# A graph network kernel: slot rows and block places fetched twice a group, and two product buffers in layer 0

## The chip, the cores and the metric

The kernel runs on 1 core of one Trainium2 chip. The metric is the device time of one execution in microseconds (us). The kernel before took 6175.32 us, the median of 6 runs (6166.19 to 6210.36).

A core has five engines that run their own instruction streams in order: PE (matrix products into PSUM; its weight loads are listed as PEld), DVE (vector work), ACT (scalar activations, copies, and here also the register work), POOL (here mainly indirect DMAs) and SP (here only DMA issues). PEq, ACTq and SPq are the sequencers of PE, ACT and SP: ACTq L1318 is a register load, SPq L1312 a DMA issue.

## The reference

Two message passing layers over the same 400,000 edges between 12,500 nodes of 32 features. The edges arrive sorted by destination. Each layer is followed by a residual sum and a layer norm.

```python
# layer 0: nine spline weights per edge, from edge_attr (two numbers per edge)
messages = jnp.einsum('ek,ei,kio->eo', basis, x[row], weight)      # 9 x 32 x 32
out = jnp.zeros(...).at[col].add(messages) / jnp.maximum(degree, 1.0)[:, None]
out = out + x @ root_w.T + root_b
x = _layernorm(x + out)
# layer 1: four weights per edge, from a table indexed by edge_type
for b in range(4):
    m = (x[src] @ W[b]) * edge_type_weight[b][edge_type][:, None]
    out = out + segment_sum(m, dst)
x = _layernorm(x + out)
```

## The kernel before

**Two ways to fetch x[src].** The edges are cut into 125 groups of 2304 (18 chunks of 128). Before the layers, the edges of each group are sorted by source on the chip. Layer 0 takes groups 33 to 124 (92 groups), layer 1 all 125: 217 in all. The rest of the edges is gathered row by row with indirect DMAs on POOL (tile `n_xg`, helper line L124): 28 gathers to a batch, one batch after the other, in both layers. This part is called "near" in the code (class `Near`).

**A group is fetched by products with one-hot matrices.** The 12,500 nodes form 98 windows of 128 nodes; 7 windows form a block, and a group has `NBL` = 14 blocks. For each block of each group there is a slot row of `WS` = 608 int16 numbers in DRAM (`slots`), which say which node of its window stands at each place. In `take(g)` the 14 blocks are cut into four `PIECES` of 3, 4, 3 and 4 blocks. For each piece, `block(k)`

- loads the slot rows into the tile `sl`, the same bytes to all 128 partitions (L1312, issued by SP);
- loads the block places, 3 or 4 int32 numbers, into `hd` on one partition (L1316, SP);
- reads these numbers into ACT's registers with one register load (L1318, ACTq TENSOR_LOAD), which is held behind the copy before last (`issue_after(moves[-2])`);
- compares the slots with the partition's own number on DVE, which gives the one-hot tile `s` (L1324).

Then for each block PE makes 7 products of node windows with the one-hot columns into one of three PSUM banks (`bank`, L1334), and ACT copies the bank into the group's row buffer `yt` at a place held in registers (L1341).

**A group is used in three steps of 6 chunks.** `use(g)` turns the rows to edges on PE (`y`, L1354) and, in `product(s)`, makes the outer products with the edge weights (tile `t`, one of `NOUT` tiles named `outer_i`; L1373 on ACT in layer 0, L584 on DVE) and the spread one-hot of the destinations (tile `hot`, a pool of `NOUT` buffers; L1374 on ACT and L1376 on DVE in layer 0, L1366 on DVE in layer 1). `add(s)` sums them on PE into `agg` (L1389); it is emitted `LAG` steps after its product. L603 copies `agg` out, L609 multiplies with the weights, L591 to L594 split the result into three bf16 parts, L746 adds them to the nodes. In layer 0 the first spline factor (`b0_ps`, L1240) lies in the same PSUM bank as `agg`.

**Buffers.** `NSRC` counts the `sl` tiles: 2 in layer 0 and 4 in layer 1, of up to 4 blocks each. `NONE` counts the `s` tiles: 3 and 5. `hd` has 2 buffers in both. Blocks of group g+1 are interleaved with the steps of group g, so fetching runs ahead of use by a group; an order within each engine is chosen by the framework's scheduler when the program is built, and each engine then runs it in order.

**Before the layers**, `counted()` works out the block places and writes them to `begin_d` in DRAM: 14 rows of 4 numbers a group, row k0 holding the places of the piece that begins at block k0 (one POOL memset, four DVE copies, one DMA).

Of the kernel before, what the change touches and what calls it, by code (L numbers as in the profile page):

```python
# [11 lines left out]
I16 = mybir.dt.int16  # L12
I32 = mybir.dt.int32
# [4 lines left out]
P = 128  # L18
# [4 lines left out]
def kernel(  # L23
# [38 lines left out]
    nc = tc.nc  # L62
# [3 lines left out]
    CH, NG, G0 = 18, 125, 33  # L66
# [29 lines left out]
    NBL = NW // B  # L96
# [13 lines left out]
    dram = ctx.enter_context(tc.tile_pool(name="dram", bufs=1, space=bass.MemoryType.DRAM))  # L110
# [21 lines left out]
    sort = phase0.enter_context(tc.tile_pool(name="sort", bufs=1))  # L132
# [45 lines left out]
    row = const.tile([P, 1], F32)  # L178
# [47 lines left out]
    def wide(name="wg"):  # L226
        return node_ps.tile([P, 4 * P], F32, name=name)
# [216 lines left out]
    WS = off_[B]  # L444
# [11 lines left out]
        signs(src_16, thr[:NG, w:w + 1], -1.0, counts[:NG, w:w + 1])  # L456

    PIECES = [(k * NBL // 4, (k + 1) * NBL // 4) for k in range(4)]
    PB = max(k1 - k0 for k0, k1 in PIECES)
    PW = PB * WS  # L460
    assert PB <= 4
    PAD = 512
    begin_d = dram.tile([NG, NBL, 4], I32, name="begin_d")
    seg = dram.tile([NG * NBL, 2], F32, name="seg")
    ROWS = TG * NBL
    NT = (NG + TG - 1) // TG
# [11 lines left out]
    def counted():  # L478
        nc.vector.tensor_scalar(counts[:NG, 1:NW], counts[:NG, 1:NW], 0.5, GE / 2, op0=ALU.mult,
                                op1=ALU.add)  # L480
        nc.vector.memset(counts[:, :1], 0.0)
        nc.vector.memset(counts[:, NW:], float(GE))
        out_, t = [sort.tile([P, NBL, B], F32, name=n) for n in ("outside", "rel_to")]
        far = sort.tile([P, 2], F32, name="far")
        firsts, ends = [counts[:NG, i:i + NW].rearrange("g (b j) -> g b j", j=B) for i in (0, 1)]
        anchors = firsts[:, :, BL:BL + 1].to_broadcast([NG, NBL, B])

        for c, to, f, op in ((firsts, out_, lo, ALU.is_lt), (ends, t, hi, ALU.is_gt)):
            nc.vector.tensor_tensor(to[:NG], c, anchors, op=ALU.subtract)
            nc.vector.tensor_tensor(to[:NG], to[:NG],  # L490
                                    f[:NG, None, :].to_broadcast([NG, NBL, B]), op=op)
        nc.vector.tensor_tensor(out_[:NG], out_[:NG], t[:NG], op=ALU.add)
        nc.vector.tensor_reduce(far[:NG, :1], out_[:NG].rearrange("g b j -> g (b j)"), axis=AX.X, op=ALU.add)
        far_ps = wide()
        nc.tensor.matmul(far_ps[:1, :1], far[:NG, :1], ones[:NG, :1], start=True, stop=True)
        nc.vector.tensor_tensor(unfit, unfit, far_ps[:1, :1], op=ALU.add)
        place = sort.tile([P, NBL], F32, name="place")
        nc.vector.tensor_tensor(place[:NG], firsts[:, :, 0], firsts[:, :, BL], op=ALU.subtract)
        nc.vector.tensor_scalar(place[:NG], place[:NG], float(AHEAD), 0.0, op0=ALU.add, op1=ALU.max)
        nc.vector.tensor_scalar(place[:NG], place[:NG], float(AHEAD), None, op0=ALU.min)  # L500

        nc.vector.scalar_tensor_tensor(place[:NG], firsts[:, :, 0], float(BANK), place[:NG],
                                       op0=ALU.mult, op1=ALU.add)
        p_i = sort.tile([P, NBL, 4], I32, name="p_i")
        nc.gpsimd.memset(p_i, 0)
        for k0, k1 in PIECES:
            n = k1 - k0
            nc.vector.tensor_copy(p_i[:NG, k0:k1, :n],
                                  place[:NG, None, k0:k1].to_broadcast([NG, n, n]))
        nc.sync.dma_start(begin_d.rearrange("g b i -> g (b i)"),  # L510
                          p_i[:NG].rearrange("g b i -> g (b i)"))
        sg = sort.tile([P, NBL, 2], F32, name="sg")
        nc.vector.tensor_scalar(sg[:NG, :, 0], firsts[:, :, BL], edges[:NG], None, op0=ALU.add)
        nc.vector.tensor_copy(sg[:NG, :, 1], node[:NG, :NW:B])
        nc.vector.tensor_scalar(sg[:NG, :, 1], sg[:NG, :, 1], row[:NG], None, op0=ALU.subtract)
        nc.sync.dma_start(seg.rearrange("(g b) i -> g (b i)", b=NBL),
                          sg[:NG].rearrange("g b i -> g (b i)"))
        nc.vector.memset(begin, 0.0)
        for t in range(NT):
            n = min(ROWS, NG * NBL - t * ROWS)  # L520
            nc.sync.dma_start(begin[:n, t, :], seg[t * ROWS:t * ROWS + n, :])
# [652 lines left out]

    def layer(which):

        NSRC, NONE, NOUT, LAG, NSUM = ((2, 3, 3, 1, 14), (4, 5, 4, 2, 18))[which]
        KK = K if which == 0 else NB
        GF = G0 if which == 0 else 0
        parts = x3[which][0]  # L1180
        with ExitStack() as stack:
            srcs = stack.enter_context(tc.tile_pool(name="srcs", bufs=NSRC))
# [3 lines left out]
            heads = stack.enter_context(tc.tile_pool(name="heads", bufs=2))  # L1186
# [112 lines left out]
            def take(g):  # L1299

                yt = yts[g % NYT]
                begins = {}
                ones_of = {}

                def block(k):
                    for k0, k1 in PIECES:
                        if k == k0:
                            n = (k1 - k0) * WS
                            sl = srcs.tile([P, PW], I16, name="sl")
                            r0 = g % TG * NBL  # L1310
                            a = slots[g // TG][r0 + k0:r0 + k1, :]
                            nc.sync.dma_start(sl[:, :n], bass.AP(tensor=a.tensor, offset=a.offset,  # L1312
                                                                 ap=[[0, P], [1, n]]))

                            hd = heads.tile([1, 4], I32, name="hd")
                            nc.sync.dma_start(hd, begin_d[g:g + 1, k0, :])  # L1316
                            with tc.issue_after(moves[-2].ins) if len(moves) > 1 else ExitStack():
                                _, v = nc.values_load_multi_w_load_instructions(  # L1318
                                    hd[:, :k1 - k0], engines=[mybir.EngineType.Activation],
                                    min_val=0, max_val=GE * BANK + AHEAD,  # L1320
                                    skip_runtime_bounds_check_because="counted, and bounded")
                            begins.update(zip(range(k0, k1), v))
                            s = ones_.tile([P, PW], BF16, name="s")
                            nc.vector.tensor_scalar(s[:, :n], sl[:, :n], row, None,  # L1324
                                                    op0=ALU.is_equal)
                            for i in range(k0, k1):
                                ones_of[i] = s[:, (i - k0) * WS:]
                    s = ones_of.pop(k)
                    bank = banks[(g * NBL + k) % len(banks)]
                    for j in range(B):  # L1330
                        a, b = at_[j]
                        w = k * B + j

                        nc.tensor.matmul(bank[:, AHEAD + a:AHEAD + b], parts[:, w * M3:w * M3 + P],  # L1334
                                         s[:, off_[j]:off_[j + 1]], start=(j == 0),
                                         stop=(j == B - 1), skip_group_check=True)
                    v = begins.pop(k)
                    to, place = [nc.s_assert_within(
                        e, 0, top, skip_runtime_bounds_check_because="counted, and bounded")
                        for e, top in ((v >> 9, GE), (v & (BANK - 1), AHEAD))]  # L1340
                    moves.append(nc.scalar.activation(  # L1341
                        yt[:M3, ds(to, LONG)], bank[:M3, ds(place, LONG)], AF.Copy))
                return [lambda k=k: block(k) for k in range(NBL)], yt

            def use(g, yt):
# [77 lines left out]
            for g in range(GF, NG + 1):  # L1423
# [6 lines left out]
                n, m = len(new), len(left)  # L1430
# [68 lines left out]
    for c in range(0, CH, 4):  # L1499
        n = min(4, CH - c)  # L1500
# [11 lines left out]
    ends[0][2].append(fallen)  # L1512
    phase0.close()
    layer(0)
    phase1.close()
    ends[1][2].append(near_fits)
    layer(1)
    again = const.tile([1, 1], I32)
    nc.vector.tensor_scalar(again, unfit, 0.5, None, op0=ALU.is_gt)
# [157 lines left out]
```

## Time and profile before

| what | value |
|---|---|
| median of 6 runs | 6175.32 us (6166.19 to 6210.36) |
| the profiled execution's own time | 6153.92 us |
| its span, first to last instruction | 6151.9 us |
| before layer 0 / layer 0 / change of layers / layer 1 | 0 to 880 / 880 to 3590 / 3590 to 3770 / 3770 to 6152 us |
| busy share of PE, PEld, DVE, ACT, POOL | 52, 44, 49, 35, 38% |
| mean granted PE clock | 0.739 of full speed |
| bytes moved by DMA | 565.07 MB, of which 511.82 MB on SP's queue |
| slot row loads | 868: 434 of 608 KB and 434 of 456 KB |
| gathers in batches | 1469 from x, 875 from `z_dram` |

A line of the groups gives the engine's busy time, the mean duration of one instruction in ns, and the idle time just before them with what ended most of it. In lines of waits the columns are: who waited at which line, for whom, us in total, times, longest. A line of a window gives its bounds, its length, the busy time and count of PE, PEld, DVE, ACT and POOL, the granted PE clock, the busy share of the 16 DMA engines and GB/s. A line of the timeline gives start, duration, engine, line, operation, tiles, count, and in brackets the idle time before it with the releaser.

### The profile page before, as it was taken

The numbers are of one execution on the slowest core, as the hardware profiler recorded it, in microseconds if no ns is written. First come the engines' busy times: TensorE is split into PE (matmuls) and PEld (weight loads), VectorE is DVE, ScalarE is ACT, GpSimd is POOL, SyncE is SP. The second block draws the span as 40 slices with busy tenths as digits, with TensorE's granted clock in tenths as the row PEclk, the third lists the DMA queues.
The fourth block names the chain that finished last, engine by engine and source line by source line (L and its number), as shares of the span: only waits on it lengthen the run. The fifth ranks groups of instructions, "written<-read, shape, count | busy, mean of one in ns | idle before, by whom it ended". The sixth has DMA issues, their size and how long they took to land.

```text
span 6151.9 us, 112981 instructions
## 1 busy us (share of the span) xinstructions
PE 3221.9 (52%) x40674; PEld 2690.5 (44%) x40674; DVE 3000.5 (49%) x5850; ACT 2154.1 (35%) x5610; POOL 2351.0 (38%) x2395
## 2 busy tenths in 40 slices
PE   1121135665556565556665664555555555555558
PEld 0111024444444444444444554555455555455547
DVE  3699685554445544334433443443443434444447
ACT  2577543333333333333333332322222223222324
POOL 5257743344433334433334213333333333333330
PEclk9955557777777777777777877777777777777779
DMA  3000023332223332222322333433333334333334
GB/s 61 6 11 15 13 86 95 94 90 86 83 84 94 91 95 82 85 81 88 89 88 78 102 112 106 126 116 114 108 117 112 110 114 121 114 114 115 118 115 144
DMA packets 266157, 565.07 MB, mean 92 GB/s; under 512 B 83608, under 2 KB 149756, under 8 KB 265086
## 3 DMA queue, kind: packets, MB, share of 16 engines
q1 hardware_dynamic: 187288, 511.82, 25.9%
q0 software_dynamic: 75888, 40.38, 4.8%
q8 instruction: 319, 5.23, 0.4%
q10 hardware_dynamic: 2410, 5.59, 0.3%
q14 instruction: 252, 2.06, 0.1%
HBM read 531.77 MB, written 25.78 MB: 91 GB/s over the span
## 4 chain that ended last, share of the span: by engine, by line
PE 37%; another core or an unknown queue 29%; issue 9%; ACT 4%; DVE 4%; DMA 1%; ACTq 1%; SPq 0%; POOL 0%; DVEq 0%
PE agg L1389 19%; PE bank L1334 12%; ACT yt L1341 2%; PE y L1354 2%; DVE outer L584 1%; PE n_bank L1083 1%; PE wg L880 1%; PE wg L609 1%; PE wg L1109 1%; DVE s L1324 1%; PE n_sum L746 1%; ACTq L1341 1%; DVE hot L1366 0%; ACT agg_sb L603 0%
## 5 line engine op out<-in xcount | busy, mean ns | idle before, releaser
L124 POOL DMA_INDIRECT n_xg<-in_x_dram,n_idx x1469 | 1479.8, 1007 | 1752.7 <-PE y L1354 453.0
L1334 PE MATMUL bank<-s,x 128*128 128x108 bf16 (+3 forms) x21266 | 1325.6, 210 | 1515.2 <-issue 903.1
L1334 PEld LDWEIGHTS <-x 128*128 128x128 bf16 x21266 | 1095.7, 103 | 1724.2 <-issue 1643.2
L1341 ACT ACTIVATE yt<-bank x3038 | 1165.9, 384 | 1667.9 <-remote 893.0
L1389 PE MATMUL agg<-hot,outer 128*128 128x82 f32 (+1 forms) x7812 | 1585.4, 347 | 238.7 <-issue 217.1
L124 POOL DMA_INDIRECT n_xg<-z_dram,near_i x875 | 842.5, 963 | 1658.1 <-PE n_bank L1083 830.3
L1389 PEld LDWEIGHTS agg<-hot,outer 128*128 128x128 f32 (+1 forms) x7812 | 1186.4, 198 | 426.6 <-issue 270.2
L1324 DVE TENSOR_SCALAR s<-sl,row 128x1824 bf16<-128x1824 int16 x868 | 669.8, 772 | 816.6 <-remote 521.3
L1366 DVE TENSOR_TENSOR hot<-in_order,y 128x492 f32<-128x492 bf16 x375 | 249.2, 665 | 691.4 <-remote 448.6
L1376 DVE TENSOR_TENSOR hot<-agg,hot_b 128x984 f32<-128x984 f32 x276 | 325.4, 1179 | 406.1 <-ACT agg_sb L603 150.4
L584 DVE TENSOR_TENSOR outer<-co,y 128x768 f32<-128x768 f32 x375 | 354.8, 946 | 0.0
L1354 PE MATMUL y<-add,yt 96*128 96x32 bf16 x3906 | 258.6, 180 | 173.6 <-DVE outer L584 115.5
L584 DVE TENSOR_TENSOR outer<-co_b,y 128x384 f32<-128x384 f32 x276 | 151.2, 548 | 311.4 <-ACT outer L1373 185.9
L1354 PEld LDWEIGHTS <-yt 96*128 96x128 bf16 x3906 | 207.9, 101 | 193.9 <-issue 187.7
L1374 ACT ACTIVATE hot<-hot_b 128x492 f32<-128x492 bf16 x276 | 167.5, 607 | 201.8 <-PE agg L1389 96.4
L1373 ACT ACTIVATE outer<-y 128x192 f32<-128x192 f32 x276 | 91.0, 330 | 405.8 <-remote 379.5
L1083 PE MATMUL n_bank<-n_w,n_xg 128*32 128x72 f32 x3024 | 112.7, 255 | 204.9 <-DVE n_w L1066 70.0
L245 ACT ACTIVATE in_order<-src,thr 125x2304 bf16<-125x2304 int16 x97 | 214.1, 2207 | 0.7
L603 ACT ACTIVATE agg_sb<-agg 128x82 f32<-128x82 f32 (+1 forms) x217 | 64.6, 298 | 416.3 <-remote 204.8
L743 DVE TENSOR_SCALAR n_hit<-cols,place_of 82x128 bf16<-82x128 f32 (+2 forms) x301 | 96.0, 331 | 198.7 <-remote 151.6
L591 ACT ACTIVATE rows<-wg 82x32 bf16<-82x32 f32 (+1 forms) x217 | 42.2, 194 | 384.6 <-remote 259.5
L609 PE MATMUL wg<-w_sb,agg_sb 97*82 97x33 f32 (+1 forms) x802 | 100.2, 245 | 139.7 <-ACT agg_sb L603 102.4
(267 smaller groups left out, 2991.6 us busy)
## 6 DMA issues: line engine op xcount, KB each, us to landing
sl<-slots SPq DMA_DIRECT2D x434, 608.0 KB
sl<-slots SPq DMA_DIRECT2D x434, 456.0 KB
n_xg<-in_x_dram,n_idx POOLq DMA_INDIRECT x1469
n_xg<-z_dram,near_i POOLq DMA_INDIRECT x875
hd<-begin_d SPq DMA_DIRECT2D x868, 0.0 KB
z_dram<-n_z SPq DMA_DIRECT2D x49, 256.0 KB
co_d<-co SPq DMA_DIRECT2D x13, 360.0 KB
co<-co_d SPq DMA_DIRECT2D x13, 360.0 KB
```

The lines of the kernel that those rows point to most:

```text
L124: return nc.gpsimd.indirect_dma_start(out=xg, out_offset=None, in_=table, in_offset=bass.IndirectOffsetOnAxis(ap=idx, axis=0))
L245: nc.scalar.activation(t, of[:NG], AF.Sign, bias=bias, scale=scale, accum_out=total)
L584: return nc.vector.tensor_tensor(t[:, :c, at:at + k * D].rearrange("p c (k d) -> p c k d", k=k), co[:, :, :, None].to_broadcast([P, c, k, D]),
L1083: nc.tensor.matmul(o, self.xg[i][:, at[0], at[1], :], v, start=True, stop=True, tile_position=(0, j * D))
L1324: nc.vector.tensor_scalar(s[:, :n], sl[:, :n], row, None, op0=ALU.is_equal)
L1334: nc.tensor.matmul(bank[:, AHEAD + a:AHEAD + b], parts[:, w * M3:w * M3 + P], s[:, off_[j]:off_[j + 1]], start=(j == 0), stop=(j == B - 1) ...
L1341: moves.append(nc.scalar.activation(yt[:M3, ds(to, LONG)], bank[:M3, ds(place, LONG)], AF.Copy))
L1354: nc.tensor.matmul(y[:, c, :], yt[:M3, k * P:(k + 1) * P], add3[:M3, :], start=True, stop=True)
L1366: nc.vector.tensor_tensor(hot.rearrange("p c (m i) -> p c m i", i=2), rel.to_broadcast([P, SUB, MAXR // 2, 2]), (col_ps if which else col_ ...
L1374: nc.scalar.activation(spread[:, :, 0, :], hot, AF.Copy)
L1376: nc.vector.tensor_tensor(spread[:, :, 1:, :], b0[:, :, :, None].to_broadcast([P, SUB, 2, MAXR]), hot[:, :, None, :].to_broadcast([P, SUB, ...
L1389: near.behind = nc.tensor.matmul(agg[0], t[:, c, :], v, start=(k == 0), stop=(k == CH - 1)).ins
```

## The change

Three things are changed.

1. Slot rows and block places are loaded in two halves of 7 blocks a group (`LOADS`), in both layers, instead of four pieces. A slot load is then 7 x 608 x 2 bytes x 128 partitions = 1,089,536 bytes, and a register load reads 7 numbers. `NSRC` is 2 in both layers, `hd` keeps 2 buffers. The one-hot compares still go by the four pieces; each reads its part of the half's tile.
2. `begin_d` becomes one row of 14 numbers a group, so the memset is dropped and one copy takes the place of four.
3. In layer 0 `NOUT` is 2 instead of 3: two tiles `outer_i` and two buffers of `hot` (the spread).

```diff
+    LOADS = [[(0, NBL // 2), (NBL // 2, NBL)]] * 2
-    begin_d = dram.tile([NG, NBL, 4], I32, name="begin_d")
+    begin_d = dram.tile([NG, NBL], I32, name="begin_d")
...
-        p_i = sort.tile([P, NBL, 4], I32, name="p_i")
-        nc.gpsimd.memset(p_i, 0)
-        for k0, k1 in PIECES:
-            n = k1 - k0
-            nc.vector.tensor_copy(p_i[:NG, k0:k1, :n],
-                                  place[:NG, None, k0:k1].to_broadcast([NG, n, n]))
-        nc.sync.dma_start(begin_d.rearrange("g b i -> g (b i)"),
-                          p_i[:NG].rearrange("g b i -> g (b i)"))
+        p_i = sort.tile([P, NBL], I32, name="p_i")
+        nc.vector.tensor_copy(p_i[:NG], place[:NG])
+        nc.sync.dma_start(begin_d[:, :], p_i[:NG])
...
-        NSRC, NONE, NOUT, LAG, NSUM = ((2, 3, 3, 1, 14), (4, 5, 4, 2, 18))[which]
+        NSRC, NONE, NOUT, LAG, NSUM = ((2, 3, 2, 1, 14), (2, 5, 4, 2, 18))[which]
...
-                ones_of = {}
+                ones_of, slots_of = {}, {}
 
                 def block(k):
-                    for k0, k1 in PIECES:
+                    for k0, k1 in LOADS[which]:
                         if k == k0:
                             n = (k1 - k0) * WS
-                            sl = srcs.tile([P, PW], I16, name="sl")
+                            sl = srcs.tile([P, max(b - a for a, b in LOADS[which]) * WS], I16, name="sl")
...
-                            hd = heads.tile([1, 4], I32, name="hd")
-                            nc.sync.dma_start(hd, begin_d[g:g + 1, k0, :])
+                            hd = heads.tile([1, NBL // 2], I32, name="hd")
+                            nc.sync.dma_start(hd[:, :k1 - k0], begin_d[g:g + 1, k0:k1])
...
                             begins.update(zip(range(k0, k1), v))
+                            slots_of.update({i: sl[:, (i - k0) * WS:] for i in range(k0, k1)})
+                    for k0, k1 in PIECES:
+                        if k == k0:
+                            n = (k1 - k0) * WS
                             s = ones_.tile([P, PW], BF16, name="s")
-                            nc.vector.tensor_scalar(s[:, :n], sl[:, :n], row, None,
+                            nc.vector.tensor_scalar(s[:, :n], slots_of[k][:, :n], row, None,
                                                     op0=ALU.is_equal)
```

## The prediction

> **What bounds the kernel now.** I first read the stages by window: two stretches without a gather batch (layer 0, layer 1), one batch of layer 1, and the stretch behind it.
>
> ```profile
> core 0: us, PE busy (x) PEld busy (x) DVE busy (x) ACT busy (x) POOL busy (x), PEclk, DMA share, GB/s
> 3509.00:3582.00 73.00, 71.20 (x901) 57.97 (x899) 50.27 (x97) 43.31 (x128) 0.00 (x0) 1.00 0.42 129
> 6004.00:6100.00 96.00, 87.33 (x1582) 83.43 (x1579) 75.78 (x138) 53.51 (x158) 0.00 (x0) 1.00 0.65 206
> 5328.00:5363.00 35.00, 5.78 (x79) 5.28 (x79) 2.69 (x6) 2.73 (x8) 26.58 (x28) 0.59 0.22 55
> 5368.00:5403.00 35.00, 31.85 (x534) 30.72 (x534) 27.23 (x50) 18.62 (x56) 0.00 (x0) 0.89 0.54 178
> ```
>
> There are two regimes. Without gathers PE is the bound: 71.2 of 73 us busy in layer 0, 87.3 of 96 in layer 1. While POOL issues its 28 gathers the rest almost stands: PE works 5.78 of 35 us, although the DMA engines are only 22% busy. From the starts of every fourth compare (L1324) I take the length of each group: without a batch 16.1 us (median of 53) in layer 0 and 10.6 us (92) in layer 1, with one 48.8 us (38) and 46.6 us (29). The 67 groups with a batch lose 38 x 32.7 + 29 x 36.0 = 2287 us. The change alters no gather, so I leave this sum alone; only what happens between batches can move.
>
> Second, the waits of the layer 1 stretch (9 groups, 36 register loads), and two of its register loads.
>
> ```profile
> ACT yt L1341 <- PE bank L1334: 16.2, 25, 1.1
> ...
> PE y L1354 <- DVE outer L584: 5.5, 5, 1.2
> ACT yt L1341 <- PE y L1354: 5.4, 14, 0.6
> ...
> ACT yt L1341 <- issue: 3.2, 5, 0.7
> ...
> PE bank L1334 <- ACT yt L1341: 2.6, 8, 0.8
> ```
> ```profile
> L1318 ACTq TENSOR_LOAD <-hd x1: 312/312/312, 4633.4 to 4633.4; - x1
> L1318 ACTq TENSOR_LOAD <-hd x1: 706/706/706, 4636.1 to 4636.1; - x1
> ```
>
> ACT mostly waits for PE (21.6 us), PE little for ACT's copies (2.6 us). The compare that starts a group or half is the 3 block one (128x1824), and counted from the first register load of layer 0 the long and the short ones alternate: the load of 3 numbers takes 0.70 us, that of 4 only 0.31. Five times in 96 us the copy behind a load came 0.64 us late with nothing else to wait for ("issue"): exactly what a 0.70 us load leaves open. So 5 of 18 long loads show on ACT.
>
> Third, the slots' transfers.
>
> ```profile
> 1423.24 0.32 SPq L1312 DMA_DIRECT2D sl<-slots  x1
> 1423.65 0.24 SPq L1316 DMA_DIRECT2D hd<-begin_d  x1
> ...
> 1426.99 0.69 DVE L1324 TENSOR_SCALAR s<-sl,row 128x1824 bf16<-128x1824 int16 x1 [0.22 <-DMA sl<-slots]
> ```
>
> This compare waited for its own transfer, so a 456 KB load takes 3.75 us from its issue. That is rare: all waits of L1324 for `sl` come to 5.8 us in 7 cases.
>
> **The change, part by part.**
>
> *Fewer loads on SP.* 434 slot issues (0.32 us) and 434 `hd` issues (0.24 us) go, 243 us of SP's time. SP ends nothing: no compare waits for an issue. A load now waits for the second compare of its half, and behind it on SP stand the `hd` load, the near part's loads (L929, L930), the stores of z (L884) and of the result (L673), and the coefficient loads; these run ahead or drain buffers that are free for some groups. Cost 0; bounds -6 us (all waits for `sl` gone) and, if a z store is late once a batch by a long compare interval, 3 us x 36 = 108 us at the worst, which I give no weight of its own.
>
> *Larger loads.* 1,089,536 bytes take the 3.75 us plus the 0.62 MB more at the rate of a busy queue: 206 GB/s at 0.65 share is 317 GB/s, so 1.96 us; together 5.7 us. Bounds: 3.75 us (size free) and 3.75 x 2.33 = 8.75 us (wholly by size). In layer 0 the time between the end of a half's second compare, which frees the buffer, and the first compare that needs it is 9.2 us or more in the stretches without gathers: covered. In layer 1 it is 5.8 to 8.9 us, median 7.5, where four quarter buffers gave a median of 9.7 from issue to use. Covered by 1.8 us at the median, 0.1 us at the worst, and a late compare would have four compares done ahead of the copies before PE feels it. Cost 0. At 8.75 us it is late by 1.25 us at the median; DVE then holds L1366 and L584, and PE's L1354 and L1389 behind them. At the start the first load lands at about 885.3 + 5.7 = 891.0, and the first compare came at 892.52: covered.
>
> *Register loads.* Per group two of 0.31 us go, two of 0.70 us (3 numbers) become loads of 7. No row shows 7 numbers. Bounds: 0.31 us (as four) and 7 x 0.70 / 3 = 1.63 us; four and three one after the other would be 1.01. Three numbers cost more than four, so the even count is the exception; I take the row of the other odd count: 1.63 us. The new wait stands in ACT's order before the copies of the half, `agg_sb` (L603), the parts (L591, L593) and, in layer 0, L1373 and L1374; for these wait PE's banks (three of them) and DVE's L1376. The load lasts 0.93 us longer. If 5 of 18 are open, that is 0.26 us of ACT each. Layer 1 has 250, of which 77% (96 of 125 groups) are outside batches: 50 us. Of this PE feels the ratio of its waits for ACT to ACT's open loads, 2.6/3.2: 40 us. Layer 0: in its stretch no copy waited for "issue", so 0 (bound: 0.26 x 184 x 0.59 = 28 us). The dropped short loads were never open: 0. The same sum at 1.01 us gives +13 us. At 0.31 us the long loads save 0.39 us each, 17 us, and at most all of PE's waits for copies end: 2.6 us in 9 groups of layer 1 and 1.3 us in 5 of layer 0, 36 + 24 = 60 us.
>
> The Trainium skill, Runtime: NRT & Kernel Launch, section Instruction fetch mechanics, gives about 200 ns for each register of such a load. By that a load of 7 would be an estimated 1.4 us and a group's 14 numbers 2.8 us before and after; the trace agrees for three numbers (0.23 us each) and not for four (0.08 us each), so the rule would put the extra at 0.7 us a long load where I have 0.93, some 30 us in all. Its page DMA: Bandwidth & Descriptors, section Rules for kernel authors, asks for 128 partitions and at least 1 MiB per DMA, which speaks for the larger loads; here the queue's rate bounds nothing, so the sum by it is 0 too.
>
> *Two product buffers in layer 0.*
>
> ```profile
> 2996.77 0.30 PE L1354 MATMUL y<-add,yt 96*128 96x32 bf16 x6
> 2996.93 2.72 PE L1389 MATMUL agg<-hot,outer 128*97 128x246 f32 x12
> 2998.59 0.32 ACT L1373 ACTIVATE outer<-y 128x192 f32<-128x192 f32 x1
> 2999.68 0.62 ACT L1374 ACTIVATE hot<-hot_b 128x492 f32<-128x492 bf16 x1 [0.77 <-PE agg L1389]
> 2999.68 1.18 DVE L1376 TENSOR_TENSOR hot<-agg,hot_b 128x984 f32<-128x984 f32 x1 [0.18 <-PE agg L1389]
> 3001.59 0.30 PE L1354 MATMUL y<-add,yt 96*128 96x32 bf16 x6
> 3001.74 2.72 PE L1389 MATMUL agg<-hot,outer 128*97 128x246 f32 x12
> ```
>
> On PE, y(s) stands before agg(s-1). With two tiles, step s overwrites what agg(s-2) read, and that ended before y(s) began, on which L1373 and L584 wait anyway. The spread (L1374, L1376) already starts only when agg(s-1) ends, because the spline factor shares its bank. Cost 0. Should the buffers bind after all, by the 0.77 us above for each of 276 steps, 59% of them outside batches: +125 us; a gain is excluded, since a buffer less releases nothing earlier.
>
> *Places.* Three DVE copies of 0.15 us and a 0.14 us memset go, at 778 us: at most 0.6 us. Cost 0.
>
> **Sum.** 6153.92 + 40 = 6194 us for the profiled execution. The median of the runs lies 21.4 us above that execution, so I say 6215 us.
>
> **Rivals.**
> - *Nothing to be seen*: a load of 7 is cheap enough (1.01 us) and ACT's waiting for PE covers it: +13 us, 6188 us. For it: 21.6 us of cover in 96. Against: the five open loads.
> - *Faster*: the load of 7 costs 0.31 us like that of four. ACT then has 1.40 us less a group, PE no longer waits for copies: between -17 and -60 us, say 6140 us. For it: the four number load. It decides from below 0.6 us a load. Against: three numbers cost 0.70.
> - *Slots late in layer 1*: a load takes nearer 8.75 us than 5.7, so its compare comes about 1 us late: 250 x 0.77 x 1 = 190 us, 6365 us. It decides from 7.5 us. For it: a DMA share of 0.65. Against: it is the upper bound.
> - *The two buffers bind in layer 0* and don't come free: 6300 us. Against: the order above.
>
> **Chances.** A measurement here tells 0.3% (18.5 us) from no change. Register loads (forecast) 0.37, own range 6194 to 6260; nothing to be seen 0.25; faster 0.25; slots late 0.09; buffers 0.04. So faster 0.25, same 0.25, slower 0.50. The range goes from 6120, near the faster case's lower end, to 6290; what lies outside is the tail of the faster case and most of the last two.
>
> **What would show it.** Right: 434 register loads, each between 1.0 and 1.7 us; more "issue" time before L1341 and more of PE's L1334 waiting for L1341 in layer 1; layer 0's stretch still over 95% PE. A load near 0.3 us makes the faster case; waits of L1324 for `sl` in layer 1 make the third; waits of L1373 or L584 for `agg` the fourth. The forecast falls altogether if the groups with a batch no longer lose 33 to 36 us, or if the scheduler's new order moves PE's work in a way that these rows don't show.

## The result and the profile after

The kernel after took 6209.6 us (median of 41 runs, 6177.22 to 6234.86), the kernel before 6187.47 us in the same series (median of 83, 6160.9 to 6212.19). The ratio is 1.0035 (95% interval 1.0026 to 1.0044): slower by some 22 us. The profiled execution of the changed kernel took 6217.3 us (span 6214.8).

First the stages by window, in the columns of before: a stretch without gathers of layer 0, one of layer 1, a batch of gathers in layer 1, and the stretch behind it.

```profile
core 0: us, PE busy (x) PEld busy (x) DVE busy (x) ACT busy (x) POOL busy (x), PEclk, DMA share, GB/s
3510.00:3583.00 73.00, 70.56 (x870) 57.43 (x870) 52.08 (x102) 42.09 (x123) 0.00 (x0) 0.95 0.47 147
6060.00:6156.00 96.00, 89.97 (x1579) 85.16 (x1579) 76.78 (x146) 52.53 (x161) 0.00 (x0) 0.98 0.65 207
5386.00:5421.00 35.00, 8.54 (x121) 7.73 (x121) 6.37 (x11) 3.56 (x11) 26.64 (x27) 0.63 0.33 89
5426.00:5461.00 35.00, 31.84 (x499) 30.58 (x499) 23.44 (x41) 15.84 (x47) 0.00 (x0) 0.86 0.47 147
```

The two regimes are still there: PE is busy for 97% of the stretch in layer 0 and 94% in layer 1, and for a quarter of a batch. From the first gather of each batch to the end of its last, batches fill 1265.1 us of layer 0 and 998.2 us of layer 1, against 1265.1 and 995.0 us before (without the one at the change of layers).

Next the waits of the stretch in layer 1 (who waited for whom, us in total, times, longest).

```profile
ACT yt L1341 <- PE bank L1334: 18.9, 18, 1.9
...
PE bank L1334 <- ACT yt L1341: 5.7, 7, 1.1
ACT yt L1341 <- issue: 5.2, 5, 1.1
...
DVE s L1324 <- DMA sl<-slots: 1.1, 2, 0.6
```

Again five copies came late with nothing else to wait for, but now by 1.04 us each where it was 0.64, and PE waited 5.7 us for copies where it was 2.6. The register load itself, from the view of the tile `hd` (durations in ns: least, median, longest):

```profile
L1314 ACTq TENSOR_LOAD <-hd x434: 956/966/1835, 913.7 to 6167.2; - x145
```

A load of 7 numbers takes 0.97 us. That is the 0.31 us of 4 numbers and 0.66 us for three more; it is far from the 1.63 us that the forecast took. In the chain of waits of layer 1 (3800 to 6060 us), first before and then after, the register load (ACTq L1314) appears, and DVE's outer products (L584 before) leave the list:

```profile
by line: another core or an unknown queue 35.2%; PE agg L1389 21.0%; PE bank L1334 17.8%; issue 10.2%; ACT yt L1341 3.2%; DVE outer L584 2.8%; PE y L1354 2.4%; PE n_bank L1083 1.2%; DVE hot L1366 1.1%; DVE s L1324 0.9%; ACT agg_sb L603 0.8%
```
```profile
by line: another core or an unknown queue 24.6%; PE bank L1334 23.9%; PE agg L1389 22.6%; issue 18.4%; ACTq L1314 3.4%; ACT yt L1341 3.4%; PE y L1354 2.5%; ACT agg_sb L599 1.1%; ACTq L1341 1.0%; PE n_bank L1079 0.8%; PE n_sum L742 0.4%; PE 
```

Over the whole execution the copies' waits with the name "issue" rise from 121.0 to 196.0 us. The compares hardly wait for slot rows (6.4 us in 13 cases, against 5.8 in 7), and the spread of layer 0 waits for the sums as before (100.0 us against 96.4):

```profile
PE bank L1334 <- ACT yt L1341: 577.8, 272, 27.8
...
ACT yt L1341 <- issue: 196.0, 137, 24.1
...
ACT hot L1374 <- PE agg L1389: 100.0, 62, 4.5
```

One thing must not be read into these two executions. The first compare of layer 0 starts at 892.5 us before and at 916.8 us after, a difference as large as the whole result. Ahead of it the changed kernel does the same sorting in the same order of DVE instructions (from 500 us on, where the shift arises), apart from the copies of the places; and in the four experiments below that ran at this pace the first compare comes at 875.5, 893.3, 906.3 and 908.8 us. The first batches of gathers fall elsewhere in the sorting in each of these executions; whether that causes the shift is not shown. Stage splits of single executions at this pace are thus uncertain by tens of us. The ratios over many runs are the measure here.

### The profile page after: what moved, and what is told of

Read it like the earlier page. It is cut to its first block, busy times and chain, and to the rows that moved or that the text cites. A ratio compares the mean times of both kernels' runs of the same rounds, so it can differ in the third digit from the quotient of the medians.

```text
span 6214.8 us, 110703 instructions
## 1 busy us (share of the span) xinstructions
PE 3278.2 (53%) x40674; PEld 2734.7 (44%) x40674; DVE 2996.9 (48%) x5847; ACT 2116.8 (34%) x5610; POOL 2346.8 (38%) x2393
## 4 chain that ended last, share of the span: by engine, by line
PE 40%; another core or an unknown queue 24%; issue 12%; ACT 4%; DVE 3%; ACTq 2%; DMA 0%; SPq 0%; POOL 0%; DVEq 0%
PE agg L1389 20%; PE bank L1334 14%; ACT yt L1341 3%; PE y L1354 2%; ACTq L1314 2%; PE n_bank L1079 1%; PE wg L876 1%; ACTq L1341 1%; PE n_sum L742 1%; PE wg L605 1%; PE wg L1105 1%; ACT agg_sb L599 0%; DVE s L1324 0%; DVE hot L1376 0%
## 5 line engine op out<-in xcount | busy, mean ns | idle before, releaser
L1334 PE MATMUL bank<-s,x 128*128 128x108 bf16 (+3 forms) x21266 | 1354.9, 211 | 1565.8 <-issue 950.8
L124 POOL DMA_INDIRECT n_xg<-in_x_dram,n_idx x1469 | 1470.8, 1001 | 1803.8 <-PE y L1354 432.4
L1334 PEld LDWEIGHTS <-x 128*128 128x128 bf16 x21266 | 1120.9, 104 | 1771.1 <-issue 1674.3
L1389 PE MATMUL agg<-hot,outer 128*128 128x82 f32 (+1 forms) x7812 | 1632.1, 351 | 282.4 <-issue 274.7
L1389 PEld LDWEIGHTS agg<-hot,outer 128*128 128x128 f32 (+1 forms) x7812 | 1218.1, 202 | 475.1 <-issue 334.2
L1354 PE MATMUL y<-add,yt 96*128 96x32 bf16 x3906 | 231.2, 180 | 51.1 <-issue 45.8
L1354 PEld LDWEIGHTS <-yt 96*128 96x128 bf16 x3906 | 194.1, 102 | 76.1 <-issue 70.3
L1062 DVE TENSOR_TENSOR n_w<-n_basis,n_hot 128x864 f32<-128x864 f32 x162 | 136.8, 850 | 57.2 <-remote 46.0
```

Of the source, the lines that this page charges most:

```text
L124: return nc.gpsimd.indirect_dma_start(out=xg, out_offset=None, in_=table, in_offset=bass.IndirectOffsetOnAxis(ap=idx, axis=0))
L1354: nc.tensor.matmul(y[:, c, :], yt[:M3, k * P:(k + 1) * P], add3[:M3, :], start=True, stop=True)
L1389: near.behind = nc.tensor.matmul(agg[0], t[:, c, :], v, start=(k == 0), stop=(k == CH - 1)).ins
```

## The experiments

Twelve kernels ran, four at a time on one chip, each with runs of the kernel before. On two of the chips the kernel before itself took 3684 and 3683 us, on the third 6120 us. The same kernel thus has two paces, which are dealt with at the end. Ratios below are to the kernel before on the same chip. The changed kernel itself ran at the quick pace (e5) and in the series of the result, but not on the chip of e9 to e12, so these are set against its 1.0035 from another chip.

| run | what differs | before, us | ratio (95% interval) |
|---|---|---|---|
| e1_two_products | before, two product buffers in layer 0 | 3684 | 0.9976 (0.9964 to 0.9989) |
| e2_places | the row of places only | 3684 | 1.0009 (0.9997 to 1.0022) |
| e3_halves_layer0 | halves in layer 0 only | 3684 | 0.9973 (0.9961 to 0.9986) |
| e4_halves_layer1 | halves in layer 1 only | 3684 | 1.0069 (1.0047 to 1.0091) |
| e5_changed_again | the changed kernel | 3683 | 1.0090 (1.0076 to 1.0105) |
| e6_places_by_half | layer 1: register loads of 7 only | 3683 | 1.0038 (1.0025 to 1.0051) |
| e7_slots_by_half | layer 1: slot rows by half only | 3683 | 1.0742 (1.0724 to 1.0760) |
| e8_four_numbers | before, two product buffers, loads of 4 | 3683 | 0.9858 (0.9844 to 0.9872) |
| e9_four_and_four | changed kernel, two loads of 4 a half | 6120 | 0.9980 (0.9954 to 1.0006) |
| e10_eight_numbers | changed kernel, one load of 8 a half | 6120 | 0.9891 (0.9859 to 0.9922) |
| e11_read_twice | changed kernel, the load of 7 called twice | 6120 | 1.0455 (1.0408 to 1.0502) |
| e12_four_three_products | before, loads of 4 | 6120 | 0.9956 (0.9935 to 0.9978) |

At the quick pace the gathers don't stop the other engines (the last section has the row). Where a stage is given, layer 0 goes from the first compare of the first group to the first compare of layer 1's fourth group, so it holds the change of layers, and layer 1 from there to the end of the last DVE instruction. Stages come from one trace each, and some are compared across the two quick chips, on which the kernel before differs by 0.9 us. What the parts cost was measured at the quick pace only; that they cost the same at the pace of the result is not shown.

**The change taken apart.** e1 is the kernel before with one number changed; e2, e3 and e4 are the changed kernel with parts undone. Halves in layer 0 leave no room for three product buffers, so e3 has two, and e4 with it.

```diff
 e1:
-        NSRC, NONE, NOUT, LAG, NSUM = ((2, 3, 3, 1, 14), (4, 5, 4, 2, 18))[which]
+        NSRC, NONE, NOUT, LAG, NSUM = ((2, 3, 2, 1, 14), (4, 5, 4, 2, 18))[which]
 e2:
+    LOADS = [PIECES, PIECES]
+        NSRC, NONE, NOUT, LAG, NSUM = ((2, 3, 3, 1, 14), (4, 5, 4, 2, 18))[which]
 e3:
+    LOADS = [[(0, NBL // 2), (NBL // 2, NBL)], PIECES]
+        NSRC, NONE, NOUT, LAG, NSUM = ((2, 3, 2, 1, 14), (4, 5, 4, 2, 18))[which]
 e4:
+    LOADS = [PIECES, [(0, NBL // 2), (NBL // 2, NBL)]]
```

> The kernel before with two instead of three product buffers in layer 0, nothing else. Theory 1 (register loads of 7 numbers, the sum on record): no change, 0 us, since a step's tiles are free before it starts. Rival 2 (the buffers bind): layer 0 longer by 15 to 25 us, ratio 1.0025 to 1.004, and layer 1 unchanged. Rival 3 (the order that a new build gives each engine): anything within 20 us, with no wait on an outer or spread tile that explains it.

> The changed kernel with loads by the four pieces, three product buffers and four slot buffers in layer 1 again, so that only the one row of places a group is left of the change. Theory 1: no change, at most 1 us, register loads of 0.31 and 0.70 us as before. Rival 2: no change. Rival 3: again anything within 20 us, though the work is the same to a few small instructions.

> The changed kernel with halves and two product buffers in layer 0 only; layer 1 loads by the four pieces into four buffers again. Theory 1: 0 to 5 us over the kernel before (layer 0 has no copy that waits for its register load). Rival 2 (buffers, or slots in layer 0): 15 to 25 us more than before, all of it between the first and the last group of layer 0. Rival 3: no relation to where the edit is.

> The changed kernel with halves in layer 1 only; layer 0 loads by the four pieces, with two product buffers. Theory 1: nearly all of the change's +22 us, ratio 1.002 to 1.004, and layer 1's stretch longer; the loads of 7 at the 0.97 us that the changed kernel's trace shows give 12 us. Rival 2: 15 to 25 us in layer 0 from the buffers and nothing in layer 1. Rival 3: no relation to where the edit is.

The places alone change nothing that can be measured. Two product buffers take 9 us off, and halves in layer 0 add nothing to that. Halves in layer 1 add 0.9% (1.0069 against 0.9976), some 34 us. Layer 0 takes 1554.6 us in e1, 1554.7 in e3 and 1552.4 in e4, and 1559.2 in e2; layer 1 takes 1338.8 us in e1, 1335.4 in e3, 1339.2 in e2 and 1374.1 in e4. So the loss sits in layer 1 alone. Rival 2 falls: e1, with two buffers, is not slower than before but 0.24% faster. In layer 1 the traces of before, e1, e2 and e3 have DVE and ACT in the same order; e4's order is another one, so rival 3 stood.

**The halves of layer 1 taken apart.** The changed kernel again, e5, and two kernels in which `LOADS` holds for the slot rows only and a second list, `PLACES`, for `hd` and the register load. Layer 0 is by pieces in both.

```diff
 e6:
+    LOADS = [PIECES, PIECES]
+    PLACES = [PIECES, [(0, NBL // 2), (NBL // 2, NBL)]]
+        NSRC, NONE, NOUT, LAG, NSUM = ((2, 3, 2, 1, 14), (4, 5, 4, 2, 18))[which]
 e7:
+    LOADS = [PIECES, [(0, NBL // 2), (NBL // 2, NBL)]]
+    PLACES = [PIECES, PIECES]
 e6, e7:
                         if k == k0:
...
                             slots_of.update({i: sl[:, (i - k0) * WS:] for i in range(k0, k1)})
+                    for k0, k1 in PLACES[which]:
+                        if k == k0:
                             hd = heads.tile([1, NBL // 2], I32, name="hd")
```

> The changed kernel itself, beside the four runs before this one: there the kernel before took 3684 us instead of 6187, two product buffers alone had a ratio of 0.998, halves in layer 1 with two product buffers 1.007. Theory 1 (register loads and what comes with the halves in layer 1): a ratio of 1.005 to 1.009 if the gathers again run through at a steady pace, 1.0026 to 1.0044 if they come in batches that hold the other engines. Rival 2 (buffers): excluded by then unless 1.01 or more. Rival 3 (order of a new build): a ratio under 1.003 on the quick pace.

> Layer 1 alone, and of the halves only the block places and their register load of 7; the slot rows stay in four pieces with four buffers. Layer 0 by pieces with two product buffers. Theory 1 (the register load): as with whole halves in layer 1, ratio 1.005 to 1.009, and idle time of ACT before the copies named issue near 106 us in the middle of layer 1. Rival 4 (slot rows by half come late or move DVE's order): no more than two product buffers alone, 0.996 to 0.999, issue near 52 us.

> Layer 1 alone, and of the halves only the slot rows in two buffers; the block places stay in four loads of 3 and 4 numbers. Layer 0 by pieces with two product buffers. Theory 1: 0.996 to 0.999. Rival 4: 1.005 to 1.009, with compares waiting for slot rows (14.8 us in the middle of layer 1 with whole halves) and fewer compares waiting for PE.

The changed kernel loses 0.9% at the quick pace, some 33 us, and all of it in layer 1: 1555.9 us for layer 0 and 1367.0 us for layer 1, where e2 had 1559.2 and 1339.2. Register loads of 7 with slot rows by pieces (e6) lose 0.6% against e1: layer 1 takes 1361.9 us, 23.1 more than in e1. The ratio of 1.0038 is under what theory 1 gave (1.005 to 1.009), and whole halves lose 0.3% more than that; the waits are of the kind that it said. Waits in the middle of layer 1 (2420 to 3600 us), first of e1, then of e6 (two lines further down in that file):

```profile
ACT yt L1341 <- issue: 53.1, 83, 1.2
...
PE y L1354 <- DVE outer L584: 50.0, 60, 1.3
...
PE bank L1334 <- ACT yt L1341: 39.4, 121, 1.1
```
```profile
ACT yt L1343 <- issue: 102.6, 96, 1.4
PE bank L1336 <- ACT yt L1343: 96.9, 110, 1.4
```

In e1 83 copies came late by 0.64 us each, 77 of them behind a load of 3 (by the order of ACT's instructions); in e6 96 by 1.07 us, 93 of them behind a load of 7. PE's waiting for copies grows by 57.5 us, and its waiting for DVE's outer products, 50.0 us in e1, is gone from e6's list, so part of the new wait stands where an old one stood. That the old one went may be due to the build's new order of instructions. The chain of waits of the same stretch puts the register load (ACTq L1317) on the path of e6:

```profile
by line: PE bank L1336 38.5%; PE agg L1391 38.0%; ACTq L1317 5.7%; ACT yt L1343 4.8%; PE y L1356 3.7%; issue 2.9%; ACT agg_sb L600 2.0%; PE n_bank L1080 1.6%; ACTq L1343 1.3%; PE n_sum L743 0.5%; DVE hot L1368 0.2%; DVE s L1326 0.2%; PE wg 
```

In e1's chain of that stretch the register load has 0.8%, in e4's and e5's 5.9% and 6.0%.

What whole halves lose beyond that may be due to slot rows that come late. In e4's stretch compares wait 14.8 us for slot rows, 19 times, and in e5's 13.6 us, 23 times; no such wait stands in the lists of e1 and e6 there. The chain of e4 shows the transfer from issue to landing:

```profile
3113.64 0.83 DVE s L1324
3114.47 0.02 issue
3114.48 7.78 DMA sl<-slots
3122.26 0.03 issue
3122.29 0.69 DVE s L1324
```

A half's slot rows took 7.78 us here, with the DMA engines busy for about 0.7 of the time (0.69 and 0.71 by the windows of e6 and e1 over this stretch), and 7.09 us at the next of these waits. These transfers hold 1.3% of e4's chain of waits, some 15 us, about what e4's layer 1 takes beyond e6's (12.2 us); in e5's chain, with the same order of layer 1, they are not among the lines listed (0.1% and more), so that this is the cause is not shown.

e7 answers no question cleanly. It lost 7.4%, but not by late slot rows: DVE's compares wait 1.5 us for them and 229 us for PE between 2420 and 3800 us. Its sequence on SP's queue is new: a half's slot load stands behind the two `hd` loads of the half before it, and an `hd` load waits for the register load two before it. SP's waits in e7 (2420 to 3600 us), where L1315 is the `hd` load and L1317 the register load:

```profile
SPq L1315 <- ACTq L1317: 570.3, 232, 5.6
SPq L1309 <- DVE s L1326: 215.7, 109, 4.5
```

In e1 these are 319.6 and 366.4 us. How that makes the engines take turns was not followed up, and part of it may be the order of that build, which is its own too: only 7 of its copies are late under "issue", where e1 has 83, with loads of the same length. Rival 4, in the form that slot rows by half come late by themselves, is neither shown nor excluded by it.

**The register load's length.** e8 and e12 read 4 numbers for every piece, with two and with three product buffers; `hd` holds a fourth number anyway. e9 and e10 keep the halves and read 8 numbers, the eighth unused, from a `begin_d` of 16 numbers a row. e11 calls the load of 7 twice. What is computed stays the same in all five.

```diff
 e8, e12:
-                                    hd[:, :k1 - k0], engines=[mybir.EngineType.Activation],
+                                    hd[:, :4], engines=[mybir.EngineType.Activation],
 e9, e10:
-    begin_d = dram.tile([NG, NBL], I32, name="begin_d")
+    begin_d = dram.tile([NG, 16], I32, name="begin_d")
...
-                            hd = heads.tile([1, NBL // 2], I32, name="hd")
-                            nc.sync.dma_start(hd[:, :k1 - k0], begin_d[g:g + 1, k0:k1])
+                            hd = heads.tile([1, 8], I32, name="hd")
+                            nc.sync.dma_start(hd, begin_d[g:g + 1, k0 + k0 // 7:k0 + k0 // 7 + 8])
 e10:
-                                    hd[:, :k1 - k0], engines=[mybir.EngineType.Activation],
+                                    hd[:, :8], engines=[mybir.EngineType.Activation],
 e9: one load of hd[:, :4] and one of hd[:, 4:]
 e11: the whole call of values_load_multi_w_load_instructions twice
```

> The kernel before with two product buffers in layer 0 and every register load of 4 numbers (the fourth unused for a piece of 3). All loads then 0.31 us instead of 0.31 and 0.70. Theory 1: faster than two product buffers alone by 434 x 0.39 us x the share that is open on ACT, some 10 to 40 us, ratio 0.985 to 0.995. Rival 3 and rival 4: as two product buffers alone, 0.996 to 0.999.

> The changed kernel, the halves as they are, but each half's 7 numbers read by two loads of 4 at the same place in ACT's stream (the eighth unused). 2 x 0.31 = 0.62 us instead of 0.97. Theory 1 (how long the register load holds ACT): all loads by fours took 1.2% off, so here at least as much off the changed kernel's 1.009: 0.988 to 1.001. Rival 3 (the halves lose by the engines' order, or by one place in ACT's stream where there were two): stays at 1.005 to 1.010, as the order and the place are those of the halves. Rival 4 (slot rows by half): 1.004 to 1.006 left, the part that halves of places alone didn't show.

> The changed kernel with one load of 8 numbers a half (the eighth unused) instead of 7. Theory 1 in the form that a load goes by fours, then a rest: 0.62 us a load and the time of the two loads of 4, 0.988 to 1.001. In the form that the time goes by the count: 1.1 us a load and 1.009 to 1.013.

> The changed kernel with every register load of 7 made twice: 434 x 0.97 = 420 us more of ACT. Theory 1: fours instead of threes and fours took 43 us for 434 x 0.39 = 169 us of ACT, so a quarter is felt: 105 us here, ratio about 1.037, 1.02 to 1.06. Rival 3 (order alone): under 1.015.

> The kernel before with every register load of 4 numbers and nothing else (three product buffers). Theory 1: 43 us less than before, ratio 0.986 to 0.990. If two product buffers are a gain of their own, 0.2% above the run with both; if not, the same 0.986.

The loads of 4 each in e8, the two loads of 4 in e9 and the load of 8 in e10, from the view of the tile `hd`:

```profile
L1318 ACTq TENSOR_LOAD <-hd x868: 304/308/741, 772.2 to 3600.5; - x174
```
```profile
L1316 ACTq TENSOR_LOAD <-hd x434: 303/308/1230, 905.8 to 6076.6; - x145
L1320 ACTq TENSOR_LOAD <-hd x434: 302/305/727, 912.0 to 6080.6; - x145
```
```profile
L1316 ACTq TENSOR_LOAD <-hd x434: 543/548/1502, 890.3 to 6016.7; - x145
```

Eight numbers cost 0.55 us, less than seven. All four kernels with shorter loads are faster than their counterparts. e8 is 1.2% (43 us) below e1, and the gain sits in layer 1: 1298.4 us against 1338.8, with layer 0 at 1554.5 against 1554.6. Against the changed kernel's 1.0035, e9 is 0.55% and e10 1.44% faster.

e11 is 4.2% (257 us) slower, but not by longer register loads. Its trace holds one load of 7 a half, as in the changed kernel; at the line of the first call only a semaphore instruction of 17 ns is left. First the two lines of the calls, then waits of layer 1 (from 3800 us on):

```profile
L1314 ACTq EVENT_SEMAPHORE  x440: 17/17/506, 902.3 to 6384.1; - x147
```
```profile
L1318 ACTq TENSOR_LOAD <-hd x434: 956/966/1628, 903.2 to 6384.5; - x145
```
```profile
PE y L1358 <- DVE outer L580: 401.9, 124, 25.8
...
ACT yt L1345 <- issue: 41.0, 19, 11.3
```

So the 420 us more of ACT that e11 was to add never ran, and that its ratio lies in the range expected is luck. Fewer copies are late than in the changed kernel (there 144.1 us, 112 times, and no wait of PE for the outer products in the list), yet layer 1 takes 2705.8 us against 2400.1. With loads of the same number and length, another order of the instructions, with one semaphore instruction more a half, moved the time by 4%. Rival 3 does not fall: e11 shows that order can weigh more than the whole change.

Each build with another load also gets another order of DVE and ACT in layer 1: before, e1, e2 and e3 share one, the changed kernel, e4 and e5 another, e8 and e12 a third, and e6, e7, e9, e10 and e11 have their own. So length and order change together in every comparison of lengths, and how much of a difference is due to which can't be parted. For the length speaks that e8, e9, e10 and e12 all gain, and that a copy behind an uncovered load is late by about the load's length: 0.26 us behind 0.31 (e8), 0.64 behind 0.70 (e1), 1.07 behind 0.97 (e6). For the order speaks, beside e11, that in e10 only 6 copies of layer 1 stand under "issue" where the changed kernel has 112, so its order covers the loads; and that in e8 (2420 to 3600 us) PE's waiting for copies falls only from 39.4 to 31.9 us, its waiting for DVE's outer products from 50.0 to 28.6. That e9 and e10 differ by 0.9%, with 0.61 and 0.55 us of load a half, is more than the length can give (434 x 0.07 = 30 us of ACT, against some 54 us). e12 gained 0.4% where 1.0 to 1.4% was expected, and layer 1 of its one trace is not shorter than before (2423.6 us against 2377.8); at its pace batches of gathers fill more than a third of the time, in which a shorter load may be worth nothing, but that was not tried by itself.

**A faster version.** The kernel before with two product buffers and loads of 4 (e8) beats both kernels at the quick pace, with a ratio of 0.9858; the changed kernel with a load of 8 (e10) beats both at the pace of the result, with 0.9891. Neither ran at the other pace, and with both the order changed too.

## Why the prediction came out as it did

The forecast was 6215 us by longer register loads in layer 1, and 6209.6 us came. The mechanism is seen in the traces: longer loads leave copies late, PE waits for them, and the load comes onto the chain of layer 1. How much of the 22 us it makes is not shown, since the order of the instructions changed with it. That the number came so near is in part luck. The sum started from 6175.32 us, and the kernel before took 6187.47 in the series of the result; the change itself was forecast at 40 us and cost 22; and two of its terms were wrong in opposite directions.

- **Batches of gathers** were left out of the sum as unaltered: their own time is, to 3 us in 2260. What they cost the groups is less so: by the prediction's count, with 14 or more gathers in a group as a batch, a group with one is longer by 31.7 us in layer 0 and 33.0 in layer 1 after (48.1 against 16.4, 44.1 against 11.1), where it was 32.7 and 36.0. The prediction named a loss outside 33 to 36 us as a sign against itself, and layer 0 lies outside; what moved it was not followed up.
- **The length of a load** was mis-sized. "I take the row of the other odd count: 1.63 us" was 0.97. By the four counts measured it is not odd or even but fours: 0.31 us for 4, 0.55 for 8, and a rest of three costs 0.66 to 0.70. The value 1.01, "four and three one after the other", stood beside the bounds and was the better choice, as it follows from the two rows together. A long load thus became longer by 0.27 us, not 0.93. The rule of the Trainium skill (Runtime: NRT & Kernel Launch, section Instruction fetch mechanics) of about 200 ns a register, which the page gives for loads from HBM where these read the tile `hd` on the core, agrees with the rest of three (0.22 to 0.23 each) and not with fours (0.07 to 0.08 each).
- **How much of it is felt** was too small. The sum had 5 of 18 loads open, 77% of layer 1 outside batches, and 0.81 of an open load felt by PE: 0.17 of each long load's extra. At the quick pace e6's layer 1 lost 23.1 us for 250 x 0.27 = 67 us, a share of 0.34, and e8's gained 40.4 us for 250 x 0.39 = 97 us, 0.41. In e1's 1180 us 77 of 222 long loads leave a copy late, 0.35 and not the 0.28 of five loads in 96 us. The two shares include whatever the builds' new orders did.
- **Layer 0: 0** for the register loads: right at the quick pace, where e3 takes as long as e1 and e8's gain is all in layer 1.
- **Larger slot loads: 0** was right where it was measured: 6.4 us of waits. At the quick pace two of the late transfers took 7.1 and 7.8 us from issue to landing instead of 5.7, inside the bounds and about the 7.5 us from which the third rival was to decide, and compares waited 14 us in 1180. The cover was thinner than the "0.1 us at the worst" as well: over all 164 cases of layer 1 before without a gather in between it is 4.7 us at the least, median 7.4. The 190 us of that rival didn't come; one load in ten was late (19 and 23 of some 216).
- **Fewer loads on SP: 0** was not tried by itself; e3, with half the loads in layer 0, takes as long as e1.
- **Two product buffers: 0**, and "a gain is excluded": no loss, as said, but e1 is 9 us faster than before, and e2's layer 0 is 4.6 us longer than e1's. Where it comes from is not shown; the order of layer 0 changed here too (e2 has that of before, e1 another). Since the scheduler sees the buffers, no gain should have been called excluded.
- **Places: 0**: e2 confirms it.

Of the rivals, "nothing to be seen" had the right price of a load (1.01 us) and gave 13 us, nearer to the measured 22 than the forecast's 40. "Faster" had the right idea of a load that costs less than it seems; e10, with a load of 8, is faster than both kernels, by its length and its order together.

## What to carry to other kernels

Read a count's price from the rows that bracket it as a sum of parts before extrapolating by parity or by size. Count the open cases over a long stretch, since a handful in one window gave 0.28 where 1180 us gave 0.35. When a build's order of instructions is free, a small edit changes that order as well: compare the order of two traces before a difference is put down to the edit, and look in the trace whether the instruction that an experiment adds is there. In e11 it was not, and the time still moved by 4%.

## What the runs showed of the hardware

**Registers load by fours, as far as four counts show.** On ACT, 3 numbers took 0.70 us, 4 took 0.31, 7 took 0.97 and 8 took 0.55, each the median of several hundred. Padding to a multiple of four made the load faster by 0.39 and 0.42 us.

**The same kernel has two paces.** On two chips the kernel before took 3684 and 3683 us, on another 6120, and 6187 where the change was measured. The windows of e2, whose work is that of before but for the places, show the quick pace in layer 1:

```profile
core 0: us, PE busy (x) PEld busy (x) DVE busy (x) ACT busy (x) POOL busy (x), PEclk, DMA share, GB/s
3000.00:3035.00 35.00, 32.23 (x581) 31.41 (x578) 27.15 (x44) 20.27 (x58) 27.38 (x26) 1.00 0.69 222
```

POOL issues 26 gathers in 35 us, as fast as in a batch of the slow pace (27 or 28), but PE is busy for 32.23 us beside them, where it was 8.54 in a batch of the changed kernel and 5.78 before. The gathers don't last longer at the slow pace (1001 and 967 ns, against 1106 and 1053 in e1); it is everything else that stands. The granted clock is 0.59 to 0.63 in the batches and 1.00 here; which of the clock and PE's idle time leads to the other is not shown. What holds the engines at the slow pace was not found.
